# A conditional transformer block on one core: another order of VectorE's sums, and the first slot tile's rows computed apart

## The chip, the cores and the metric

The kernel runs on one core of a Trainium2 chip. The metric is the device time of one execution in microseconds (us), taken as the median over several runs. The profile is one more execution, traced instruction by instruction. Engines are named as in the profile: PE is TensorE (matmul, with its weight loads as PEld), DVE is VectorE, ACT is ScalarE, POOL is GpSimd, SP is SyncE, which here only issues DMAs.

## The reference

All data is float32: `x` is [32, 128, 512] (batch, token, feature), `cond` is [32, 512], the mask is [32, 128]. In short form:

```
shift, scale, gate = split(silu(t) @ ada_w + ada_b)          # per batch
norm = where(m, layernorm(x) * (1 + scale) + shift, 0)
ssm  = gelu(norm @ ssm_w1 + b1) @ ssm_w2 + b2  +  gelu(norm @ bwd_w1 + ..) @ bwd_w2 + ..   # exact gelu
x    = x + gate * where(m, ssm, 0)
shift, scale, gate = split(silu(t) @ ffada_w + ffada_b)
h    = gelu_tanh((layernorm(x) * (1 + scale) + shift) @ ff_w1 + ff_b1)     # 512 -> 1024
out  = x + gate * (h @ ff_w2 + ff_b2)                                      # 1024 -> 512
```

The flip of the sequence around the second network has no effect, since each token is treated alone. Only masked tokens go through the first half; in these inputs they are few.

## The kernel before, in words

**Order.** The whole body stands under a manual schedule: each engine runs its instructions in the order in which the code issues them. So where a line stands in the code, or under which key it is put in a table of fills, decides what it waits behind. Every wait is on a semaphore that the producing engine raises; an instruction that waits holds back all that follows on its engine.

**The head (up to about 84 us).** The masked tokens are counted on the chip and given 512 slots, four tiles of 128 (a loop at the end would take any further ones). The head computes the modulation rows `mod1` of all batches (PE, L309, copied out of PSUM by DVE in `modulation_rows`, L320), picks the rows of the first two slot tiles with matmuls (`of_slots`, L333: tile 0 and tile 1 in the same PSUM banks, one bank for each quarter of the features), and gathers the tokens of the slots. For each of the two tiles c = 0, 1 DVE then computes the mean and variance (L158, L159, L161), POOL the reciprocal root (L163), and DVE the modulated rows in two passes over four strips (`modulated_by_strips`, L347 and L351). Between the two tiles DVE also turns counts into the token numbers of the last two slot tiles (`counted`, L260 to L269), which read the result of two matmuls of `slots_to_count` (L254). PE transposes a tile in four steps (`transposed_slots`, L193) and ACT copies it to SBUF in two halves (L196). After a small transpose `ptr_b` (L684, L685), the first network's matmuls start (`ph_s`, L673). While PE has nothing to do in this stretch, it is given matmuls whose result nobody reads: `keep_clock(2, 0)` (L620, eight matmuls) and two with the identity (L647). SP issues the loads of the weights; `ssm_w1` is one load of 1 MB behind the first gather.

**The second half, four pairs.** The 32 batches are taken in NP = 4 pairs, each of two sides of G = 4 batches. Both matmul layers are done by a seven-product scheme of the Strassen kind, applied twice to the first layer. `FirstProduct` runs seven streams in the order 1, 2, 5, 6, 3, 7, 4, each with its products P5, P1, P3, P7, P2, P6, P4. A window (w = 1 to 6) interleaves the beginning of a new stream with the end of the old one. Each product is 4 passes of a 128x256 matmul in the trace (L1117). Each product goes into one of two accumulators, the banks `e` and `a`; DVE or ACT then reads the bank and forms the next partial sum. The DVE lines are:

- L1142, `seed`: e = a + an earlier result, at P1;
- L1147 (P7) and L1152 (P4): result = a + a stored part, into `hb`;
- L1161: e = a + p5 or a stored part, at P6.

PE can use the bank again only when that DVE line has read it. Line numbers as the profile has them: where a DVE line is the continuation of a statement, its number is that of the call.

**The token sums.** The streams 5, 6, 3, 7, 4 use sums and differences of blocks of the transposed input. `token_sums(j, n)`, j = 1 to 4, n = 0 to 3, forms them on DVE: j = 1 at L1046 (`sx`), j = 2 at L1050 (`xn_sy`), j = 3 at L1053 and j = 4 at L1056, both in place. In pair 0 all of j = 2 and (3, 0) stand ahead of the windows and the others at (2, 1) to (2, 6), that is, after the second to seventh product of window 2. In pairs 1 to 3 (2, 0) stands in the pair before, at the last step, and the others in windows 1 and 2.

**Beside them on DVE** stand the statistics of the next pair (`Statistics.one`, L917 and L918; `root`, L922, and on POOL L923), one small difference `fb2_step` (L1433), and after the windows `blocks(0, i)`: normalise a tile of the next pair (L929) and turn it in 32x32 blocks (L1479). POOL does the additions of the first layer (L1168, L1197, L1201) and issues the gathers of corrected tokens (`take_first_half`, L885). The second layer is `SecondProduct` (L1304) with steps in the order P1U, P5U, P1V, ... P4V; its `first_block` is DVE L1251.

The fills are put in by pairs of keys, window and product number:

```
for n, at in enumerate(((2, 1), (2, 3), (2, 3))):
    put(*at, now.token_sums, 3, 1 + n)
```

Of the kernel before, what the change touches and what calls it, by code (L numbers as in the profile page):

```python
# [9 lines left out]
F32 = mybir.dt.float32  # L10
# [12 lines left out]
def kernel(  # L23
# [111 lines left out]
    def load_behind_gathers(t, w):  # L135
        nc.gpsimd.memset(t[0:1, 0, 0:1], 0.0)
        load_blocks(t, w)
# [48 lines left out]
        nc.vector.scalar_tensor_tensor(t, t, stats[1], shift, ALU.mult, ALU.add)  # L186
        return t

    def transposed_slots(xn, dst, name):

        ptr = ps_t.tile([P, 512], F32, tag="tr", name=f"ptr_{name}")
        for k in range(KC):
            nc.tensor.transpose(ptr[:, ts(k, P)], xn[:, ts(k, P)], ident)  # L193
        for half_no in range(2):
            k = ts(half_no, KC // 2)
            nc.scalar.copy(dst[:, k], ptr.rearrange("p (k s) -> p k s", s=P)[:, k])  # L196

    def hidden(xT, n, w, bcol, func, name, pool, parts=range(HC), after=None):

# [47 lines left out]
            pick[:, part], slot_row[:, part], first, inside[:, part], ALU.is_ge, ALU.mult  # L247
        )

    def slots_to_count(picked, n, name, bank):  # L250

        pl = bank[0].tile([P, 512], F32, tag=bank[1], name=f"pl_{name}")
        for c in range(n):
            nc.tensor.matmul(pl[:, ts(c, S)], picked[:B, ts(c, P)], rank, start=True, stop=True)  # L254
        return pl[:, : n * S].rearrange("p (c s) -> p c s", s=S)

# [61 lines left out]
    def modulation_rows(pm, mod, lo, hi):  # L318
        view = pm[:, : (hi - lo) * P].rearrange("p (m c) -> p m c", c=P)
        nc.vector.tensor_copy(mod[:, lo:hi], view)  # L320

    def of_slots(picked, tiles, mod, kinds, banks, name):

        n = kinds.stop - kinds.start
        t = [
            pool.tile([P, 512], F32, tag=tag, name=f"{name}_{j}")[:, : len(tiles) * n * P].rearrange(
                "p (a m c) -> p a m c", m=n, c=P
            )
            for j, (pool, tag) in enumerate(banks)
        ]  # L330
        for at, c in enumerate(tiles):
            for j in range(KC):
                nc.tensor.matmul(  # L333
                    t[j][:, at],
                    picked[ts(j, B), ts(c, P)],
                    mod[ts(j, B), kinds],
                    start=(at == 0),
                    stop=True,
                    skip_group_check=True,
                )  # L340
        return t
# [243 lines left out]
    for c, bank in enumerate(((ps_o, "o"), (ps_t, "tr"))):  # L585
        if c:
            on_zeros(256)
        slot = slot_col[:, c : c + 1]
        token_c = tokens_of(pick[:, ts(c, P)], slot, 1, f"s0_{c}", ssm, bank)
        xc.append(both[:, c])  # L590
        gather(xc[c], token_c)
        if c == 0:
            load_behind_gathers(w1[:, :, :D], ssm_w1)
    load_behind_gathers(ada_a[:, :, 2 * D :], ada_w[:, 2 * D :])
    load_blocks(w1[:, :, D:], bwd_w1)
    raw = [x_tile(2 * n, 2) for n in range(2 * G // 2)]
# [31 lines left out]
    pm = ps_o.tile([P, 512], F32, tag="o", name="pm_ss")  # L628
    modulation_bias(pm, AT_A, 0, 2)
    modulation_matmuls(pm, ada_a, 0, 2, range(KC))  # L630
    slots_of_late = slots_to_count(pick[:, NH:], NC // 2, "s1", (ps_h, "h"))
    modulation_rows(pm, mod1, 0, 2)

    strips = of_slots(pick, (0, 1), mod1, slice(0, 2), 3 * [(ps_o, "o")] + [(ps_h, "h")], "part_s0")
    keep_clock(2, 0)
    xT_s = ssm.tile([P, KC, NH], F32, tag="xT", name="xT_s0", bufs=2)
    xT_t = ssm.tile([P, KC, NH], F32, tag="xT", name="xT_s1", bufs=2)
    xn = group_of_tiles("s")
    xn_s = []
    for c in range(2):  # L640
        mv, rstd = statistics(xc[c : c + 1], f"s{c}")
        xn_s.append(
            modulated_by_strips(xc[c], strips, c, xn[:, c], mv[:, 0, 0:1], rstd, xn[:, 2 + c])
        )
        if c == 0:
            for n in range(2):
                nc.tensor.matmul(  # L647
                    pm_keep_clock[:, ts(n, 2 * P)], ident, xn[:, 2, ts(n, 2 * P)], start=True, stop=True
                )
            token_i = counted(slots_of_late, slot_col[:, NC // 2 :], NC // 2, "s1", ssm)  # L650
    gather_slots(token_i)
    one_more_scale(AT_F)
    fw1 = fwp.tile([P, KC, FF], F32, name="fw1")
# [25 lines left out]
                skip_group_check=True,  # L679
            )  # L680

    transposed_slots(xn_s[0], xT_s[:, :, ts(0, P)], "s0")
# [737 lines left out]
    for n in range(2, 4):  # L1420
        now.token_sums(1, n)
    now.do(2, "P2", "P6")
    for n in range(4):
        now.token_sums(2, n)
    now.do(1, "P4")
    now.token_sums(3, 0)
    for p in range(NP):
        more_pairs = p + 1 < NP
        xs = x_of[p]
# [2 lines left out]
        def put(w, n, f, *args):  # L1432
            fills.setdefault(w, {}).setdefault(n, []).append(lambda: f(*args))  # L1433

        if p:
            for n, at in enumerate(((1, 3), (1, 4), (1, 6))):
                put(*at, now.token_sums, 2, 1 + n)
            put(1, 6, now.token_sums, 3, 0)
        for n, at in enumerate(((2, 1), (2, 3), (2, 3))):
            put(*at, now.token_sums, 3, 1 + n)  # L1440
        for n, at in enumerate(((2, 4), (2, 4), (2, 6), (2, 6) if more_pairs else (3, 1))):
            put(*at, now.token_sums, 4, n)
        put(3, 6, now.load_weights, 3)
        if p == 0:
            put(3, 6, load_rows_of_fw2, 0)
# [5 lines left out]
        second = SecondProduct(p, now.h, xs)  # L1451
        if p == 0:
            put(
                2, 0, nc.vector.tensor_tensor,
                fb2_step, fb2[:, D // 2 :], fb2[:, : D // 2], ALU.subtract,
            )
        put(6, 0, now.late_gelu, "11")
# [7 lines left out]
        if more_pairs:  # L1465
            x_next = x_of[p + 1]
            stats = [Statistics(x_next[side], f"{p + 1}_{side}") for side in range(2)]
            xn, xT = {}, {}

            def blocks(side, i):  # L1470

                if i == 0:
                    xn[side] = in_turned_blocks(
                        group_of_tiles(f"{p + 1}_0")
                        if side == 0
                        else sp.tile([P, G, D], F32, tag="s12", name=f"xn_{p + 1}_1")
                    )
# [48 lines left out]
        if more_pairs:  # L1526

            for i in range(G):
                put(2 + i // 2, blocks, 1, i)
            for k in range(KC):  # L1530
                put(4 + k // 2, lambda k: scaled(2 * (p + 1), xT[0], k), k)
                put(7 + k // 2, lambda k: scaled(2 * (p + 1) + 1, xT[1], k), k)
                if k == 1:
                    put(4, to_feature_rows, 1, nc.sync, nc.sync, nc.sync, nc.scalar)

            def begin(j):
                if j == 1:
# [12 lines left out]
            nxt = {}  # L1550
            put(10, next_product)
            put(11, lambda: nxt["p"].do(1, "P5", "P1"))
            for n in range(4):
                put(11 + n // 2, lambda n: nxt["p"].token_sums(1, n), n)
            put(13, lambda: nxt["p"].token_sums(2, 0))
            if p + 2 < NP:
                x_of[p + 2] = [[], []]
                put(11, lambda: x_of[p + 2][0].extend(load_side(p + 2, 0)))
            put(12, lambda: nxt["p"].do(1, "P2", "P6"))
            put(13, lambda: nxt["p"].load_weights(2))  # L1560
            if p + 2 < NP:
                put(13, lambda: x_of[p + 2][1].extend(load_side(p + 2, 1)))
# [128 lines left out]
```

## Time and profile before

| | us |
|---|---|
| median of 3 runs (456.37 to 456.99) | 456.78 |
| the profiled execution | 455.45 |
| its span, first to last instruction | 453.7 |
| PE busy, 2151 rows | 446.6 |
| DVE busy, 571 rows | 331.7 |
| ACT busy | 178.0 |
| POOL busy | 159.8 |

The profiled execution has 1.75 us around its span. The granted clock of TensorE has a mean of 0.999. In the timeline view each row gives the start, the duration, the engine, the line and operation, the operands and how many instructions were put together (x4); in brackets stands how long the engine had been idle before it and what ended that. The durations of matmul groups include their draining, so that the rate is read from start to start: a group of 4 passes that follows another without a pause starts 0.86 to 0.87 us after it.

### The profile page before, as it was taken

Reading aid. Unit: us, or ns where it says so; the run is one execution under the profiler, and the core shown is the slowest. Engines: PE = TensorE matmul, PEld = TensorE weight load, DVE = VectorE, ACT = ScalarE, POOL = GpSimd, SP = SyncE. Lnnn points to the kernel's source line nnn. Section 1 sums busy time; section 2 is a strip of 40 time slices with the busy share of each in tenths; the row PEclk is TensorE's granted clock in tenths of the full one; section 3 lists DMA queues with packets and bytes.
Section 4 is the critical chain, followed back from the end, with each engine's and each line's share of the span. In section 5 each row is a group of like instructions: output and inputs, shape, how many; then the busy total and the mean of one; then the engine's idle time right before and its main releaser. Section 6 shows DMA issues by size and latency. Waiting matters only on the chain.

```text
span 453.7 us, 6170 instructions
## 1 busy us (share of the span) xinstructions
PE 446.6 (98%) x2151; PEld 370.4 (82%) x2151; DVE 331.7 (73%) x571; ACT 178.0 (39%) x390; POOL 159.8 (35%) x154
## 2 busy tenths in 40 slices
PE   8999999999999999999999999999999999999996
PEld 3884585688888888888888888888888888888885
DVE  5798797697789759886796498867963995534645
ACT  3124127244642552446425514454355154552000
POOL 4220550089770000797700007977000027560000
PEclk9999999999999999999999999999999999999999
DMA  7999449745518817722187167221872442222023
GB/s 251 379 396 407 150 73 326 279 151 172 189 78 180 114 49 251 249 92 82 66 191 107 56 230 264 95 84 54 202 105 59 157 145 82 81 94 93 0 82 107
DMA packets 82611, 70.57 MB, mean 156 GB/s; under 512 B 63112, under 2 KB 63728, under 8 KB 81554
## 3 DMA queue, kind: packets, MB, share of 16 engines
q1 hardware_dynamic: 67762, 58.28, 40.9%
q0 software_dynamic: 4160, 10.54, 6.9%
q10 hardware_dynamic: 10656, 1.33, 2.1%
q8 instruction: 18, 0.29, 0.2%
q14 instruction: 15, 0.12, 0.1%
HBM read 56.46 MB, written 13.70 MB: 155 GB/s over the span
## 4 chain that ended last, share of the span: by engine, by line
PE 92%; DVE 5%; POOL 1%; issue 1%; ACT 1%; DVEq 0%
PE a_o L1304 23%; PE a_m L1117 18%; PE e_o L1304 18%; PE e_m L1117 14%; PE po_s L221 6%; PE ph_s L204 5%; PE ph_s L673 2%; PE pm_ss L309 1%; PE last L1304 1%; PE pm_f L309 1%; PE a_m_alone L1117 1%; PE pl_s L254 1%; DVE xn_sy L1050 0%; PE part_s L333 0%; DVE e_m L1142 0%
## 5 line engine op out<-in xcount | busy, mean ns | idle before, releaser
L1168 POOL TENSOR_TENSOR ha<-p_m,ha 128x512 f32<-128x512 f32 x20 | 25.8, 1289 | 178.8 <-ACT ha L1175 169.2
L1304 PE MATMUL e_o<-fw,ha 128*128 128x256 f32 x256 | 57.9, 379 | 0.0
L939 ACT ACTIVATE xT<-xT,modT 128x128 f32<-128x128 f32 x112 | 44.1, 480 | 31.6 <-DMA xT<-xn 31.4
L1304 PE MATMUL a_o<-t,hb 128*128 128x256 f32 x240 | 54.1, 379 | 0.0
L1304 PEld LDWEIGHTS e_o<-fw,ha 128*128 128x128 f32 x256 | 48.6, 190 | 6.6
L1304 PEld LDWEIGHTS a_o<-t,hb 128*128 128x128 f32 x240 | 45.6, 190 | 6.2
L1079 ACT ACTIVATE hb<-hb,biasT 128x256 f32<-128x256 f32 x64 | 29.0, 500 | 30.4 <-POOL hb L1201 19.8
L1131 ACT COPY p_m<-e_m 128x512 f32<-128x512 f32 x27 | 15.8, 586 | 47.8 <-PE e_m L1117 43.3
L885 POOL DMA_INDIRECT x<-x_rows,slot_i x24 | 29.2, 1218 | 6.0 <-issue 5.3
L1168 POOL TENSOR_TENSOR hb<-p_m,hb 128x512 f32<-128x512 f32 x20 | 29.6, 1481 | 0.3
L1304 PE MATMUL a_o<-fw,ha 128*128 128x256 f32 x128 | 28.9, 379 | 0.0
L1304 PE MATMUL a_o<-t,s 128*128 128x256 f32 x128 | 28.9, 379 | 0.0
L1304 PE MATMUL e_o<-fw,s 128*128 128x256 f32 x128 | 28.9, 379 | 0.0
L221 PE MATMUL po_s<-w,h_s 128*128 128x512 f32 x64 | 28.4, 594 | 0.0
L1175 ACT COPY ha<-e_m 128x512 f32<-128x512 f32 x32 | 18.5, 578 | 24.9 <-PE e_m L1117 24.6
L1304 PEld LDWEIGHTS a_o<-t,s 128*128 128x128 f32 x128 | 24.3, 190 | 3.3
L1304 PEld LDWEIGHTS a_o<-fw,ha 128*128 128x128 f32 x128 | 24.3, 190 | 3.3
L1304 PEld LDWEIGHTS e_o<-fw,s 128*128 128x128 f32 x128 | 24.3, 190 | 3.3
L1142 DVE TENSOR_TENSOR e_m<-a_m,ha 128x512 f32<-128x512 f32 x20 | 13.9, 696 | 17.0 <-POOL ha L1168 6.6
L1079 ACT ACTIVATE ha<-e_m,biasT 128x256 f32<-128x256 f32 x48 | 20.0, 468 | 14.8 <-PE e_m L1117 12.6
L1117 PE MATMUL a_m<-xT,tw 128*128 128x256 f32 x96 | 24.7, 380 | 0.4 <-DVE hb L1147 0.4
L1117 PE MATMUL e_m<-s,fw 128*128 128x256 f32 x92 | 23.8, 381 | 0.0
(237 smaller groups left out, 892.3 us busy)
## 6 DMA issues: line engine op xcount, KB each, us to landing
tw<-t_rows SPq DMA_DIRECT2D x16, 896.0 KB, 5.3
x<-in_x_dram SPq DMA_DIRECT2D x16, 512.0 KB, 8.8
gate<-gate_rows POOLq DMA_DIRECT2D x8, 1024.0 KB, 5.2
out_dram<-x SPq DMA_DIRECT2D x15, 512.0 KB, 4.9
xT<-xn SPq DMA_DIRECT2D x92, 64.0 KB, 2.4
ada_f<-in_L_cond_ffada_w_dram SPq DMA_DIRECT2D x4, 768.0 KB, 13.2
ada_a<-in_L_cond_ada_w_dram SPq DMA_DIRECT2D x4, 512.0 KB
w<-in_L_cond_ssm_w_dram SPq DMA_DIRECT2D x2, 1024.0 KB, 6.2
```

The costliest lines, as they stand in the source:

```text
L204: nc.tensor.matmul(ph[:, :n], w[:, k, ts(f, P)], xT[:, k, :], start=(k == 0), stop=(k == KC - 1))
L221: nc.tensor.matmul(po, h[f][:, ts(i, P)], w[:, f, :], start=(f == 0 and seeded is None), stop=(f == HC - 1), skip_group_check=seeded is no ...
L309: nc.tensor.matmul(pm[ts(j, B), : (hi - lo) * P], sT[:, k, :], kinds[:, k, lo:hi, ts(j, P)], start=False, stop=True, skip_group_check=True,)
L885: nc.gpsimd.indirect_dma_start(out=xs[i // G][i % G // 2][:, i % 2], out_offset=None, in_=x1_rows, in_offset=bass.IndirectOffsetOnAxis(ap= ...
L939: nc.scalar.activation(out, src, AF.Identity, bias=shift, scale=scale)
L1079: nc.scalar.activation(dst[:, n], src[:, n], AF.Gelu_apprx_tanh, bias=biasT[:, f : f + 1])
L1117: nc.tensor.matmul(bank[:, ts(n, QT)], self.w_block(j, product)[:, ts(n, P)], self.x_block(j, product), start=(product in ("P1", "P5") and ...
L1131: nc.scalar.copy(p5, e)
L1142: nc.vector.tensor_tensor(e, a, p5, add)
L1168: nc.gpsimd.tensor_tensor(self.place(RESULT[j], c), self.p5[j], other, ALU.add)
L1175: nc.scalar.copy(self.place(RESULT[j], c), src)
L1304: nc.tensor.matmul(part, src[:, k, ts(i, P)], w[product][:, k, :], start=(last and k == 0), stop=True, skip_group_check=True,)
```

## The change

In the head:

- The modulation rows are copied by ACT.
- The parts of slot tile 0 alone (`parts_of_tile(0)`, four matmuls) are issued between the two matmuls of `slots_to_count`, those of tile 1 after the transposes of tile 0.
- The transposes of tile 0 stand ahead of the work for tile 1, in two PSUM tiles of two transposes each, so that each of ACT's two copies has its own.
- `keep_clock` has four matmuls instead of eight, and the matmul with the identity stands once instead of twice.
- `ssm_w1` is loaded in two halves of 0.5 MB. SP so issues one DMA more.

In the pairs:

- The token sums of pair 0 are spread to later windows; in pairs 1 to 3 all of j = 2 stands in window 1, with nothing of it in the pair before.
- `fb2_step` moves from (2, 0) to (4, 1).
- The statistics of the next pair's side 0 move to later products, by one in pairs 1 and 2 and by three in pair 0; the root of side 0 moves from (3, 6) to (4, 1) in pairs 1 and 2, and one statistic of side 1 from (4, 6) to (5, 1).
- In pair 0, `blocks(0, 1)` moves behind the stream's P7.

On the engines this leaves DVE with one instruction fewer, ACT with one more, PE with five matmuls fewer (the keep-clock ones), and the number of POOL's unchanged.

```diff
-    def transposed_slots(xn, dst, name):
-        ptr = ps_t.tile([P, 512], F32, tag="tr", name=f"ptr_{name}")
+    def transposed_slots(xn, dst, name, apart=False):
+        ptr = [ps_t.tile([P, 512], F32, tag="tr", name=f"ptr_{name}")]
+        if apart:
+            ptr.append(ps_t.tile([P, 512], F32, tag="tr", name=f"ptr_{name}_1"))
         for k in range(KC):
-            nc.tensor.transpose(ptr[:, ts(k, P)], xn[:, ts(k, P)], ident)
+            nc.tensor.transpose(ptr[k // 2 % len(ptr)][:, ts(k, P)], xn[:, ts(k, P)], ident)
         for half_no in range(2):
             k = ts(half_no, KC // 2)
-            nc.scalar.copy(dst[:, k], ptr.rearrange("p (k s) -> p k s", s=P)[:, k])
+            t = ptr[half_no % len(ptr)]
+            nc.scalar.copy(dst[:, k], t.rearrange("p (k s) -> p k s", s=P)[:, k])
...
         for c in range(n):
+            if c and between:
+                between()
             nc.tensor.matmul(pl[:, ts(c, S)], picked[:B, ts(c, P)], rank, start=True, stop=True)
...
-            load_behind_gathers(w1[:, :, :D], ssm_w1)
+            load_behind_gathers(w1[:, :, : D // 2], ssm_w1[:, : D // 2])
+            load_blocks(w1[:, :, D // 2 : D], ssm_w1[:, D // 2 :])
...
-    slots_of_late = slots_to_count(pick[:, NH:], NC // 2, "s1", (ps_h, "h"))
-    modulation_rows(pm, mod1, 0, 2)
-    strips = of_slots(pick, (0, 1), mod1, slice(0, 2), 3 * [(ps_o, "o")] + [(ps_h, "h")], "part_s0")
-    keep_clock(2, 0)
+    def parts_of_tile(c):
+        strips_of[c] = of_slots(
+            pick, (c,), mod1, slice(0, 2), 3 * [(ps_o, "o")] + [(ps_h, "h")], f"part_s{c}"
+        )
+    nc.scalar.copy(mod1[:, 0:2], pm.rearrange("p (m c) -> p m c", c=P)[:, 0:2])
+    slots_of_late = slots_to_count(
+        pick[:, NH:], NC // 2, "s1", (ps_h, "h"), lambda: parts_of_tile(0)
+    )
+    keep_clock(1, 0)
...
+    modulated_slots(0)
+    nc.tensor.matmul(pm_keep_clock[:, : 2 * P], ident, xn[:, 2, : 2 * P], start=True, stop=True)
+    transposed_slots(xn_s[0], xT_s[:, :, ts(0, P)], "s0", True)
+    parts_of_tile(1)
+    token_i = counted(slots_of_late, slot_col[:, NC // 2 :], NC // 2, "s1", ssm)
+    modulated_slots(1)
...
-    for n in range(4):
+    for n in range(2):
         now.token_sums(2, n)
     now.do(1, "P4")
-    now.token_sums(3, 0)
...
+        sums = [(j, n) for j in (2, 3, 4) for n in range(4)]
         if p:
...
+            at_sums = (
+                (1, 1), (1, 3), (1, 4), (1, 6), (1, 6), (2, 1), (2, 3), (2, 3),
+                (2, 4), (2, 4), (2, 6), (2, 6) if more_pairs else (3, 1),
+            )
+        else:
+            sums = sums[2:]
+            at_sums = (
+                (2, 1), (2, 3), (2, 3), (2, 4), (2, 4), (2, 6), (3, 1), (3, 1), (3, 3), (3, 3),
+            )
...
-                2, 0, nc.vector.tensor_tensor,
+                4, 1, nc.vector.tensor_tensor,
                 fb2_step, fb2[:, D // 2 :], fb2[:, : D // 2], ALU.subtract,
...
-            for i, at in enumerate(((3, 1), (3, 3), (3, 4), (3, 6))):
+            for i, at in enumerate(((3, 1), (3, 3), (3, 4), (4, 1)) if p else ((3, 4), (3, 6), (4, 1), (4, 3))):
                 put(*at, stats[0].one, i)
-            put(*((3, 6) if p else (5, 4)), stats[0].root)
-            for i, at in enumerate(((4, 4), (4, 6), (5, 3), (6, 4))):
+            put(*((4, 1) if p else (5, 4)), stats[0].root)
+            for i, at in enumerate(((4, 4), (5, 1), (5, 3), (6, 4))):
...
-            for i in range(2):
+            for i in range(1 + (p > 0)):
                 blocks(0, i)
         now.do(4, "P3")
         second.seed(1)
         now.do(4, "P7")
+        if more_pairs and p == 0:
+            blocks(0, 1)
...
-            put(13, lambda: nxt["p"].token_sums(2, 0))
```

More of the change, by code (lines that the diff above doesn't have):

```diff
@@ L248, in pick_slots, with slots_to_count @@
         )
-    def slots_to_count(picked, n, name, bank):
+    def slots_to_count(picked, n, name, bank, between=None):
         pl = bank[0].tile([P, 512], F32, tag=bank[1], name=f"pl_{name}")
         for c in range(n):
+            if c and between:
+                between()
             nc.tensor.matmul(pl[:, ts(c, S)], picked[:B, ts(c, P)], rank, start=True, stop=True)
@@ L630 @@
     modulation_matmuls(pm, ada_a, 0, 2, range(KC))
-    slots_of_late = slots_to_count(pick[:, NH:], NC // 2, "s1", (ps_h, "h"))
-    modulation_rows(pm, mod1, 0, 2)
-    strips = of_slots(pick, (0, 1), mod1, slice(0, 2), 3 * [(ps_o, "o")] + [(ps_h, "h")], "part_s0")
-    keep_clock(2, 0)
+    strips_of = {}
+    def parts_of_tile(c):
[7 more added lines that the diff above has]
+    keep_clock(1, 0)
     xT_s = ssm.tile([P, KC, NH], F32, tag="xT", name="xT_s0", bufs=2)
@@ L639, with modulated_slots @@
     xn_s = []
-    for c in range(2):
+    def modulated_slots(c):
         mv, rstd = statistics(xc[c : c + 1], f"s{c}")
         xn_s.append(
-            modulated_by_strips(xc[c], strips, c, xn[:, c], mv[:, 0, 0:1], rstd, xn[:, 2 + c])
+            modulated_by_strips(xc[c], strips_of[c], 0, xn[:, c], mv[:, 0, 0:1], rstd, xn[:, 2 + c])
         )
[L645 to L650, printed above, removed]
+    modulated_slots(0)
[4 more added lines that the diff above has]
+    modulated_slots(1)
     gather_slots(token_i)
@@ L680, in hidden_of_tile @@
             )
-    transposed_slots(xn_s[0], xT_s[:, :, ts(0, P)], "s0")
     ptr = ps_t.tile([P, 512], F32, tag="tr", name="ptr_b")
@@ L1433, in put @@
             fills.setdefault(w, {}).setdefault(n, []).append(lambda: f(*args))
+        sums = [(j, n) for j in (2, 3, 4) for n in range(4)]
         if p:
[L1436 to L1442, printed above, removed]
+            at_sums = (
[7 more added lines that the diff above has]
+            )
+        for at, of in zip(at_sums, sums):
+            put(*at, now.token_sums, *of)
         put(3, 6, now.load_weights, 3)
```

## The prediction

> **What bounds the kernel now.** The page's first part and its chain that ended last are read first.
>
> ```profile
> PE 446.6 (98%) x2151; PEld 370.4 (82%) x2151; DVE 331.7 (73%) x571; ACT 178.0 (39%) x390; POOL 159.8 (35%) x154
> ...
> PE 92%; DVE 5%; POOL 1%; issue 1%; ACT 1%; DVEq 0%
> ```
>
> TensorE is busy 98% of the span and makes 92% of the chain. So only its remaining pauses, or matmuls taken from its queue while nothing else holds it, can give time. Such a pause is short, so the second view is the waits of PE: it names `a_m L1117 <- DVE hb L1147` with 0.7 us in two waits. Busy time hides more than this, so the third view is PE's timeline, read from start to start: a group of 4 passes should start 0.865 us after the one before.
>
> ```profile
> 97.75 1.03 PE L1117 MATMUL a_m<-sx,tw 128*128 128x256 f32 x4
> 99.00 1.13 PE L1117 MATMUL a_m<-xT,t 128*128 128x256 f32 x4 [0.23 <-DVE hb L1147]
> 99.97 1.03 PE L1117 MATMUL e_m<-xn_sy,tw 128*128 128x256 f32 x4
> 100.83 1.03 PE L1117 MATMUL a_m<-xn_sy,tw 128*128 128x256 f32 x4
> 101.75 1.13 PE L1117 MATMUL e_m<-sx,tw 128*128 128x256 f32 x4
> 102.72 1.03 PE L1117 MATMUL a_m<-sx,tw 128*128 128x256 f32 x4
> 103.88 1.13 PE L1117 MATMUL e_m<-xn_sy,tw 128*128 128x256 f32 x4
> ```
>
> Three groups come late: 99.00 by 1.25 - 0.865 = 0.39, 101.75 by 0.06, 103.88 by 0.30. The group after each pause also takes 0.97 instead of 0.865 to its successor, 0.10 more each time. Together: 0.39 + 0.06 + 0.30 + 3 x 0.10 = **1.05**. What came late is on DVE's timeline:
>
> ```profile
> 96.73 0.68 DVE L1053 TENSOR_TENSOR s<-s 128x512 f32<-128x512 f32 x1
> 97.33 0.41 DVE L1433 TENSOR_TENSOR fb_step<-fb 128x256 f32<-128x256 f32 x1
> 97.67 0.67 DVE L1053 TENSOR_TENSOR xT<-xT 128x512 f32<-128x512 f32 x1
> 98.27 0.67 DVE L1147 TENSOR_TENSOR hb<-a_m,hb 128x512 f32<-128x512 f32 x1
> ...
> 102.81 0.41 DVE L1056 TENSOR_TENSOR s<-s,xn_sy 128x256 f32<-128x256 f32 x1
> 103.14 0.68 DVE L1161 TENSOR_TENSOR e_m<-a_m,ha 128x512 f32<-128x512 f32 x1
> ```
>
> DVE has no pause from 91.65 to 108.3. The read of PE's bank (L1147, L1161) stands behind token sums and `fb2_step`, and PE starts 0.06 us after that read ends (98.94 to 99.00, 103.82 to 103.88).
>
> **The change part by part.**
>
> *Pair 0, token sums.* Eight sums (7 of them 0.67 or 0.41 long) leave the stretch from 95 to 103, `fb2_step` (0.41) too. Up to the L1147 of 98.27 DVE had four sums of j = 2 (0.68, 1.28 for two, 0.41), three of j = 3 and `fb2_step` since 94.59, 3.7 us of work behind each other. In the new order only (2,0) and (2,1) (about 1.3) and two or three more stand before it, and PE's product for it ends at about 97.0: the read goes then, 1.2 us earlier. The L1161 of 103.14 likewise stands behind at most two sums per product, about 1.2 us against the 0.865 to 1.73 us that PE gives between two reads. So all three pauses go: **-1.05**. The sums are wanted later than they come: the latest, (4,3) at (3,3), is read by a stream that starts a window (7 x 0.865 = 6 us) later. The statistics of side 0 (four of 0.68 + 0.18) that move back fall where DVE waits 0.6 to 1.05 us for others at a time (rows at 110.23, 112.79, 116.34). The same holds for `fb2_step`, which is first read by the `seed` of the second layer more than 15 us later.
>
> *Pair 0, `blocks(0, 1)`.* A second place of the same kind:
>
> ```profile
> 129.89 3.62 PE L1304 MATMUL e_o<-fw,s 128*128 128x256 f32 x16
> 133.93 1.13 PE L1117 MATMUL a_m<-xT,tw 128*128 128x256 f32 x4 [0.42 <-DVE hb L1147]
> ```
>
> 16 passes are 4 x 0.865 = 3.46, so 133.35 was due and 133.93 came: 0.58, and 0.10 behind it. DVE's L1147 (133.22, 0.65 long) stands behind two normalisations and two turns (130.07 to 133.2). With only one pair ahead of it it starts at about 131.3 and ends at 132, before PE asks: **-0.68**. The moved pair (1.27 + 0.64) then runs from 132 to 134, and the L1152 of 135.59 is behind it as before. The chain for the next pair (DVE's turned rows, SP's DMAs, ACT, DVE's L986) ends at 166.83 and PE takes it at 169.59, 2.8 us of slack, of which PE's own gain takes little, since DVE's last turned row moves with PE.
>
> *Pairs 1 to 3.* At 206.59 to 207.63, 297.55 to 298.58 and 364.30 to 365.35 PE waits for the L1161 of 206.89, 297.85 and 364.61; each interval is 1.04, 1.03 and 1.05, so 0.17 + 0.17 + 0.18 late and 0.10 behind each. In pairs 1 and 2 a statistic (206.07 and 297.03, 0.68 + 0.18) stands ahead of it, in pair 3 (2,0) at 364.00 (0.68). All three are moved behind: **-0.82**. The root of the next pair's side 0 moves on POOL behind two L1168 (1.26 each); the sum that follows (L1197, 203.58) comes at the same time, as the three only change places. The whole of j = 2 in window 1 is done there between reads, where in pairs 1 and 2 DVE waits 0.9 to 1.8 us (rows at 201.58 and 204.87).
>
> *The head.*
>
> ```profile
> 12.35 1.02 PE L333 MATMUL part_s<-mod,pick 32*128 32x256 f32 x13
> 13.41 1.12 DVE L347 SCALAR_TENSOR_TENSOR xn_s<-xc,mv_s,part_s 128x128 f32<-128x128 f32 x4 [0.38 <-PE part_s L333]
> ...
> 16.46 3.81 PE L673 MATMUL ph_s<-xT_s,w 128*128 128x128 f32 x32 [0.27 <-issue]
> ```
>
> DVE waits for the last of eight matmuls (13.37). ACT's copy of the rows costs 0.37 (its rows at 20.75) where DVE's took 0.42, so the parts may start at 12.0; four of the eight end 0.6 earlier, at 12.8. L347 then starts 0.58 earlier, and so the transposes. From there PE has the parts of tile 1 (4 matmuls; eight take 1.07 at 25.99, so 0.54 to 0.64) and `ptr_b` between the transposes and L673, where it had only `ptr_b`. With the transposes' end at about 15.3 these end at 15.9 and `ptr_b` at 16.15. The matmul chain wants the first of ACT's two copies only, and this waits for two transposes instead of four (15.3 instead of 15.99). So L673 starts at 16.15: **-0.31**; bounds are -0.58 (nothing added on PE's path) and +0.1 (parts of tile 1 wait for the strips of tile 0). The five keep-clock matmuls taken away (0.13 to 0.28 each) fell into waiting time and give nothing. The DMA more costs SP 0.43 to 0.68 of issue (rows at 15.96 and 10.00); `ssm_w1`'s bytes are the same, and the second half is wanted 1.8 us after the first, so nothing. `counted` moves from before L158 of tile 1 to the same place after tile 0: nothing; tile 1's rows are ready at 19.0 and wanted at 19.8.
>
> Sum: -1.05 - 0.68 - 0.82 - 0.31 = **-2.86**. Not every wait can go entirely, as POOL's case below says; I take -2.8. The profiled execution's 455.45 becomes 452.65. It lies 1.33 below the median of the runs, 456.78, which so becomes **454.0**. About 0.2% (0.91 us) is what a measurement of this kernel can tell from no change: below 455.87 counts as faster.
>
> **A rule against it.** In pair 0 the gathers of POOL at 99.89 and 102.26 take 2.07 and 1.83 against 1.00 for others, and L1168 1.71 (92.08) against 1.27, each while DVE adds two SBUF tensors; DVE's own sum at 92.58 takes 1.48 against 0.42. [...]
>
> **Rivals.**
>
> *A: POOL takes DVE's place in pair 0.* POOL works without a pause from 93.94 to 114. L1142 at 112.79 follows POOL's L1197 (111.48 + 1.27 = 112.75), and PE takes its bank at 114.35 with 0.8 us to spare. If PE comes 1.05 earlier and POOL doesn't, PE waits 0.27 there, and 0.10 behind it: -2.49, 454.3. If moved sums also slow POOL's additions (0.44 each, as at 92.08, in three of them), all of pair 0's 1.05 is handed back: -1.81, 455.0. For it: the unbroken row. Against it: the gathers get shorter when DVE's sums leave them (2 x 0.9).
>
> *B: the wait goes to the next in line.* DVE's work is the same in sum; what is moved delays another bank read as much. Then pairs 0 to 3 give nothing and blocks(0, 1) its 0.68: 456.1, no change. Against it: DVE waits at most of the places to which work moves.
>
> *C, slower: TensorE's clock.* Less filler in the head: PE has pauses of about 0.3 each near 13.5 and 14. If the granted clock fell to half there, all of PE's work from 14.3 to 20.1 (0.93 + 1.00 by the windows to 16.5, 3.60 to 20.1) would take twice as long: +5.5 - 2.86 = +2.7, 459.4. It decides from 2.9 us of matmuls at half the clock. Against it: PE's weight loads show 0.90 without work at 10.45, and the windows from 11.3 to 16.5 and to 20.1 have 1.00. [...]
>
> **How the numbers follow.** Forecast (453.2 to 454.3): 0.55. A (454.3 to 455.2): 0.23. B (455.9 to 456.5): 0.11. C: 0.06. The other 0.05: half of it gains above 3.5 (the -0.58 of the head's bound, waits that I count at nothing), half a loss of unknown place. The range 453.0 to 455.6 holds forecast and A with their bounds. Faster: 0.55 + 0.23 + 0.025 = 0.81; same 0.11; slower 0.08.
>
> **What would show it.** In the changed kernel: no gap over 0.9 between groups of 4 passes near 98 to 104 and 133, the L1161 of pairs 1 to 3 directly behind L1152, L673 at about 16.15, clock 1.00 from 11 to 20. A shows as a new wait of PE near 113 for L1142 with POOL's L1197 before it. Wrong would be: the same intervals of 1.05 to 1.25 at other places, or a later L673.

## The result, and the profile after

The changed kernel takes 460.72 us (median of 6 runs, 458.79 to 461.95), the kernel before in the same comparison 456.31 (6 runs, 455.51 to 456.99): ratio **1.009**, 95% interval 1.0072 to 1.0108. By this ratio it is slower by about 4.1 us (the medians lie 4.4 apart); forecast were 454.0 and a range of 453.0 to 455.6. The profiled execution took 460.46, its span is 458.7 beside 453.7 of before, 5.0 more.

One correction to the text on record: in the description of the kernel before, L1142 and L1161 are exchanged (L1161 is `seed` at P1, L1142 the sum at P6); no number depends on it.

In the changed kernel these lines stand 14 further down: the read at P7 is L1161 (L1147 before), `seed` L1175, the sum at P6 L1156, the sums of j = 4 L1070; POOL's additions are L1182 and L1211, its gathers L899. In experiments with two lines added, L1211 is L1213 and `fb2_step` (L1446) is L1448. The views leave out numbers in tile names, so `fb2_step` reads `fb_step`.

The page, its first part and the chain that ended last:

```profile
PE 448.9 (98%) x2141; PEld 371.3 (81%) x2141; DVE 337.2 (74%) x570; ACT 178.9 (39%) x391; POOL 160.1 (35%) x154
...
PE 72%; DMA 8%; DVE 5%; SPq 4%; ACT 4%; POOL 4%; issue 3%; ACTq 0%; POOLq 0%; DVEq 0%
```

DVE has one instruction fewer than before and is busy 5.5 us longer (331.7 before): something made single instructions longer. PE has lost 20 points of the chain. PE's waits name the place:

```profile
PE a_m L1131 <- DVE hb L1161: 3.1, 1, 3.1
```

PE's timeline there (start, duration, operation, in brackets the idle time before it):

```profile
97.96 1.03 PE L1131 MATMUL a_m<-sx,tw 128*128 128x256 f32 x4
98.82 1.03 PE L1131 MATMUL a_m<-xT,t 128*128 128x256 f32 x4
99.68 1.03 PE L1131 MATMUL e_m<-xn_sy,tw 128*128 128x256 f32 x4
...
103.14 1.03 PE L1131 MATMUL e_m<-xn_sy,tw 128*128 128x256 f32 x4
104.00 1.03 PE L1131 MATMUL a_m<-xn_sy,tw 128*128 128x256 f32 x4
108.15 2.08 PE L1131 MATMUL a_m<-sx,tw 128*128 128x256 f32 x4 [3.12 <-DVE hb L1161]
110.02 1.53 PE L1131 MATMUL e_m<-s,fw 128*128 128x256 f32 x4
111.39 1.03 PE L1131 MATMUL a_m<-xT,fw 128*128 128x256 f32 x4
```

The three pauses between 98 and 104 are gone, as forecast. Then 4.15 us lie between two starts where 0.865 were due, and the two groups behind take 1.87 and 1.37 each. DVE and POOL in the same stretch:

```profile
101.68 0.70 DVE L1175 TENSOR_TENSOR e_m<-a_m,ha 128x512 f32<-128x512 f32 x1
102.29 4.61 DVE L1070 TENSOR_TENSOR s<-s,xn_sy 128x512 f32<-128x512 f32 x1
106.82 0.68 DVE L1070 TENSOR_TENSOR xT<-xT,xn_sy 128x512 f32<-128x512 f32 x1
107.42 0.68 DVE L1161 TENSOR_TENSOR hb<-a_m,p_m 128x512 f32<-128x512 f32 x1
```

```profile
101.47 1.12 POOL L899 DMA_INDIRECT x<-x_rows,slot_i  x1 [0.30 <-issue]
102.62 1.28 POOL L1182 TENSOR_TENSOR ha<-p_m,ha 128x512 f32<-128x512 f32 x1
103.84 1.28 POOL L1182 TENSOR_TENSOR hb<-p_m,hb 128x512 f32<-128x512 f32 x1
105.07 1.26 POOL L1211 TENSOR_TENSOR ha<-ha 128x512 f32<-128x512 f32 x1
106.49 1.30 POOL L899 DMA_INDIRECT x<-x_rows,slot_i  x1 [0.16 <-issue]
```

The sum (4,0) takes 4.61 us where its like takes 0.68. It begins under a gather, and ends 0.57 us (106.90) after the last of three POOL additions (106.33), which themselves take 1.26 to 1.28 each, as three in a row did in the kernel before (104.11 to 107.83). The windows view (stretch, length, busy time with count for PE, PEld, DVE, ACT, POOL, granted clock, DMA share, GB/s) shows the second part of the price, a granted clock of 0.50 behind the pause:

```profile
105.00:108.00 3.00, 0.03 (x1) 0.00 (x0) 3.00 (x3) 0.00 (x0) 2.63 (x3) 0.94 0.00 0
108.00:109.00 1.00, 0.85 (x2) 0.76 (x3) 1.00 (x4) 0.00 (x0) 0.00 (x0) 0.50 0.12 33
109.00:110.00 1.00, 1.00 (x3) 0.75 (x3) 0.97 (x4) 0.00 (x0) 0.00 (x0) 0.50 0.00 0
110.00:111.00 1.00, 1.00 (x4) 0.80 (x3) 1.00 (x2) 0.59 (x1) 0.00 (x0) 0.50 0.00 0
111.00:112.00 1.00, 1.00 (x6) 0.90 (x5) 0.25 (x2) 0.36 (x1) 0.00 (x0) 0.99 0.80 151
```

**Where the 5.0 us come from**, by the start of the same matmul in both traces (minus is earlier than before). The table compares one execution of each kernel:

| place (time before) | step, us | stands at |
|---|---|---|
| head, L673 at 16.46 | -0.66 | -0.66 |
| 34 to 39.4: gates, second matmuls of the first half | +0.87 | +0.21 |
| pair 0 to 104.2: the three pauses | -1.06 | -0.85 |
| 105.7: wait for the held sum | +3.29 | +2.44 |
| 105.7 to 107.4: half clock | +1.51 | +3.95 |
| up to 118.7 | +0.32 | +4.27 |
| 133.9: `blocks(0, 1)` | -0.69 | +3.58 |
| 134.9: seed of the second layer | +0.49 | +4.07 |
| pair 1: 203.1 and 207.6 | +0.25, -0.31 | +4.01 |
| pair 2: 294.1 and 298.6 | +0.24, -0.30 | +3.95 |
| pair 3: 351 to 370 | +1.03 | +4.98 |

### The profile page after: what moved, and what is told of

Read it like the earlier page. It is cut to its first block, busy times and chain, and to the rows that moved or that the text cites. A ratio compares the mean times of both kernels' runs of the same rounds, so it can differ in the third digit from the quotient of the medians.

```text
span 458.7 us, 6152 instructions
## 1 busy us (share of the span) xinstructions
PE 448.9 (98%) x2141; PEld 371.3 (81%) x2141; DVE 337.2 (74%) x570; ACT 178.9 (39%) x391; POOL 160.1 (35%) x154
## 3 DMA queue, kind: packets, MB, share of 16 engines
q10 hardware_dynamic: 10656, 1.33, 2.1%
## 4 chain that ended last, share of the span: by engine, by line
PE 72%; DMA 8%; DVE 5%; SPq 4%; ACT 4%; POOL 4%; issue 3%; ACTq 0%; POOLq 0%; DVEq 0%
PE a_m L1131 17%; PE a_o L1318 17%; PE e_m L1131 14%; PE e_o L1318 13%; PE po_s L224 5%; DMA w<-in_L_cond_bwd_w_dram 4%; SPq L970 3%; PE ph_s L207 3%; DMA ada_a<-in_L_cond_ada_w_dram 2%; DMA xT<-xn 1%; ACT xT L953 1%; POOL hb L1215 1%; PE last L1318 1%; PE a_m_alone L1131 1%; POOL ha L1215 1%
## 5 line engine op out<-in xcount | busy, mean ns | idle before, releaser
L1182 POOL TENSOR_TENSOR ha<-p_m,ha 128x512 f32<-128x512 f32 x20 | 26.3, 1317 | 182.8 <-ACT ha L1189 169.1
L953 ACT ACTIVATE xT<-xT,modT 128x128 f32<-128x128 f32 x112 | 44.2, 480 | 34.6 <-DMA xT<-xn 34.0
L1182 POOL TENSOR_TENSOR hb<-p_m,hb 128x512 f32<-128x512 f32 x20 | 29.8, 1492 | 0.3
L899 POOL DMA_INDIRECT x<-x_rows,slot_i x24 | 27.8, 1159 | 6.0 <-issue 5.3
L1093 ACT ACTIVATE ha<-e_m,biasT 128x256 f32<-128x256 f32 x48 | 20.1, 469 | 14.9 <-PE e_m L1131 13.5
L1156 DVE TENSOR_TENSOR e_m<-a_m,ha 128x512 f32<-128x512 f32 x20 | 13.9, 697 | 14.3 <-POOL ha L1182 6.6
```

The costliest lines, as they stand in the source:

```text
L899: nc.gpsimd.indirect_dma_start(out=xs[i // G][i % G // 2][:, i % 2], out_offset=None, in_=x1_rows, in_offset=bass.IndirectOffsetOnAxis(ap= ...
L953: nc.scalar.activation(out, src, AF.Identity, bias=shift, scale=scale)
L1093: nc.scalar.activation(dst[:, n], src[:, n], AF.Gelu_apprx_tanh, bias=biasT[:, f : f + 1])
L1156: nc.vector.tensor_tensor(e, a, p5, add)
L1182: nc.gpsimd.tensor_tensor(self.place(RESULT[j], c), self.p5[j], other, ALU.add)
```

## The experiments

**Theory 1:** POOL's additions hold a VectorE sum that reads two SBUF tensors, and the new order in pair 0 brings such a sum to them. **Theory 2:** the time is lost in the head or the later pairs, or the sum waits for something of its own. Ratios are against the kernel before, run beside each.

**Pair 0 as before, all else changed.** The sums, `fb2_step` and side 0's statistics of pair 0 get their old places; the first five of these sums (`sums[:5]`) stand ahead of the windows again:

```diff
...
-            sums = sums[2:]
-            at_sums = (
-                (2, 1), (2, 3), (2, 3), (2, 4), (2, 4), (2, 6), (3, 1), (3, 1), (3, 3), (3, 3),
-            )
+            sums = sums[5:]
+            at_sums = ((2, 1), (2, 3), (2, 3), (2, 4), (2, 4), (2, 6), (2, 6))
...
```

> The changed kernel, with the order of pair 0's token sums, of fb2_step and of its side-0 statistics as before; all else as changed. Theory 1 (POOL's additions hold a VectorE sum that reads two SBUF tensors): the sum (4,0) no longer meets three additions in a row, so the 4.61 us row at 102.29 is gone, and with it 3.29 us of PE pause and 1.5 us at half the clock; the 1.05 us that the order had gained before that place are lost. 460.7 - 4.8 + 1.05 = 457.0, with no L1070 row over 1 us and a granted clock of 1.00 from 84 to 160. Theory 2 (the head or the later pairs cost the time): stays near 460.

Measured: 455.97 beside 455.96, ratio 0.9993 (0.9979 to 1.0008), clock 1.00, no L1070 row above 1 us in pair 0. The whole loss is in pair 0's order. All other parts of the change together are worth nothing that can be measured. I had expected 457.0, which is 0.7 above the 456.31 of the kernel before; no such difference was measured.

**Pair 0's order alone, on the kernel before** (the same edit the other way round; the sums of j = 4 are L1056 here).

> The kernel before with only pair 0's order of token sums, fb2_step and side-0 statistics as in the change. Theory 1: the same meeting of (4,0) with three additions: -1.05 + 3.3 + 1.5 = +3.7 on 456.3, so 460.0, with one L1056 row of 3 to 5 us and a stretch of half clock behind it. Theory 2 (head or later pairs): about 455.3 with no such row.

Measured: 460.83 beside 455.96, ratio 1.0121 (1.0085 to 1.0156). Its L1056 at 102.20 takes 4.59 us, PE's wait is 3.1 and the clock 0.50 from 109 to 111. Both directions agree.

**Gathers between the additions.** DVE's order is that of the change; one gather moves between the two L1182 of stream 6, one ahead of L1211:

```diff
             nc.gpsimd.tensor_tensor(self.place(RESULT[j], c), self.p5[j], other, ALU.add)
+            if self.p == 0 and j == 6 and c == "12":
+                take_first_half(1, x_of[1], range(G + 1, G + 2))
...
-            put(2, 6, take_first_half, p + 1, x_next, range(G, G + 2))
-            put(3, 4, take_first_half, p + 1, x_next, range(G + 2, G + 3))
+            put(2, 6, take_first_half, p + 1, x_next, range(G, G + 2 if p else G + 1))
+            put(3, 4 if p else 2, take_first_half, p + 1, x_next, range(G + 2, G + 3))
```

> The changed kernel with VectorE's order untouched; of POOL's gathers in pair 0 one is put between its two L1182 additions of stream 6, and one before its L1211, so that no two additions stand next to each other there. Theory 1: the sum (4,0) gets through in the first gap, after one addition at most: its row takes 0.7 to 1.9 us instead of 4.61, PE's pause is under 0.4, the clock stays at 1.00: 460.7 - 4.5 = 456.2 (455.8 to 457.0). Theory 2 (the sum is held by something that it alone waits for, such as its operands or a load into SBUF in that stretch): the row stays at 4.6 and the time at 460.7.

Measured: 459.14, ratio 1.0061 (1.0040 to 1.0083): half right. DVE's timeline, and POOL's behind it:

```profile
101.38 1.12 DVE L1070 TENSOR_TENSOR s<-s,xn_sy 128x512 f32<-128x512 f32 x1
...
108.39 3.02 DVE L1448 TENSOR_TENSOR fb_step<-fb 128x256 f32<-128x256 f32 x1
```

```profile
104.86 1.29 POOL L899 DMA_INDIRECT x<-x_rows,slot_i  x1 [0.16 <-issue]
106.17 1.29 POOL L1213 TENSOR_TENSOR ha<-ha 128x512 f32<-128x512 f32 x1
107.40 1.28 POOL L1182 TENSOR_TENSOR ha<-p_m,ha 128x512 f32<-128x512 f32 x1
108.62 1.27 POOL L1182 TENSOR_TENSOR hb<-p_m,hb 128x512 f32<-128x512 f32 x1
109.85 1.26 POOL L1213 TENSOR_TENSOR ha<-ha 128x512 f32<-128x512 f32 x1
```

The sum (4,0), the first row, gets through in 1.12 instead of 4.61, as theory 1 says and theory 2 denies. But now another sum with two SBUF inputs, the moved `fb2_step`, meets the next run of additions, and is held until they end (111.11): 3.02 instead of 0.41. PE waits 2.0 us for the read behind it, and the clock is 0.50 from 113 to 116.

**Both holds taken away:** the edit above, and `fb2_step` early, where POOL is idle:

```diff
     for n in range(2):
         now.token_sums(1, n)
+    nc.vector.tensor_tensor(fb2_step, fb2[:, D // 2 :], fb2[:, : D // 2], ALU.subtract)
     now.apart(1)
...
-        if p == 0:
-            put(
-                4, 1, nc.vector.tensor_tensor,
-                fb2_step, fb2[:, D // 2 :], fb2[:, : D // 2], ALU.subtract,
-            )
```

> The changed kernel with POOL's gathers between its additions as above, and fb2_step early (behind the first two token sums), so that neither (4,0) nor fb2_step meets a run of additions. Theory 1: the pause of 2.0 us at 112.86, the slow clock behind it and the 0.4 us at 107.10 go too, and the whole loss of the change with them: 455.2, between 454.5 and 456.0, granted clock 1.00 from 84 to 160, no two-input sum over 1.8 us. Rival (pair 0's new order costs something else besides): above 456.5.

Measured: 455.35 beside 455.86, ratio 0.9984 (0.9957 to 1.0011). The loss of the change is gone with the two holds; what is left of its gain is within the noise.

**The sums of j = 4 later.** The four go from (3,1) and (3,3) to (3,3) and (3,4), behind the bank read.

> The changed kernel with the four sums of j = 4 of pair 0 put one or two products later: (4,0) and (4,1) behind the bank read at (3,3), (4,2) and (4,3) at (3,4). Theory 1: the sums start while POOL's additions run already (102.6 to 106.3). If additions in a row hold any sum until the last of them is done, (4,0) still ends at about 106.9, but the bank read is ahead of it, so PE loses only what stands behind: the next read of a bank or the sum itself, wanted at about 105.7; 458 to 459.5. If a sum takes turns with the additions, as at 92.29 to 94.3, each of the four takes 1.0 to 1.8 us, the last ends near 107.5: 456.5 to 457.5. Theory 2 (held by its operands): a row near 4.6 or none, at no fixed place against POOL.

Measured: 457.46, ratio 1.0035 (1.0017 to 1.0054). The sum (4,0) starts at 104.62, 0.10 us into the second of three additions, and is held 2.95 us, to 0.57 after the third:

```profile
104.62 2.95 DVE L1070 TENSOR_TENSOR s<-s,xn_sy 128x512 f32<-128x512 f32 x1
```

So in both traces the hold ended with the run of additions (0.57 us behind its end), whether the sum began 0.33 us ahead of the first of them or 0.10 into the second. The bank read is ahead of it, PE waits 0.9 and 1.1 us in two pieces, and the clock stays at 1.00. The time lies in the range that I had given for sums that take turns (456.5 to 457.5) and below the one for the hold (458 to 459.5); the row of 2.95 us decides for the hold.

**Do sums and additions take turns or not?** Elsewhere in the same traces they do (in the kernel before `sx` at 92.58 takes 1.48 us instead of 0.42, and the L1168 beside it 1.71 instead of 1.27). Three kernels measure it: behind step 3 of the second layer POOL gets a run of additions, released by one DVE instruction, and DVE four instructions beside it (all in addition to the kernel before). They ran once each, and only their rows are read. The first:

```diff
...
+                nc.vector.tensor_tensor(met, fb2, fb2, ALU.add)
+                for _ in range(6):
+                    nc.gpsimd.tensor_tensor(met, met, fb2, ALU.add)
+                for n in range(4):
+                    if p == 0:
+                        nc.vector.tensor_tensor(by[:, :256], fb2[:, 256:], fb2[:, :256], ALU.subtract)
+                    elif p == 1:
+                        nc.vector.tensor_scalar(by[:, :256], fb2[:, :256], 1.0, None, ALU.add)
+                    else:
+                        nc.vector.bn_stats(st, fb2)
...
```

> The kernel before with added work that leaves the output as it is: behind step 3 of the second layer in pairs 0, 1 and 2 POOL does six additions in a row (128x512, two SBUF inputs, released by one VectorE instruction), and VectorE four instructions beside them: in pair 0 sums with two SBUF inputs (128x256, 0.41 us alone), in pair 1 one-input tensor_scalars of that size, in pair 2 one-input statistics (0.68 alone). Theory 1 (POOL's additions in a row hold a sum with two SBUF inputs): in pair 0 the first sum lasts until the sixth addition ends, about 7.6 us, and the additions take 1.26 each; if instead they take turns, each of the four sums takes 1.0 to 1.7 and the additions about 1.7. In pair 2 neither engine is slowed. For pair 1 I have no firm expectation: 0.3 us each if one input never meets, or held as in pair 0 if it does.

```profile
143.74 4.64 DVE L1574 TENSOR_TENSOR by<-fb 128x256 f32<-128x256 f32 x4
...
238.08 4.28 DVE L1576 TENSOR_SCALAR by<-fb 128x256 f32<-128x256 f32 x4
...
331.91 2.88 DVE L1578 BATCH_NORM_STATS2 st_met<-fb 128x6 f32<-128x512 f32 x4
```

Theory 1 in my form is wrong here: they take turns. Three of the four sums took 1.37 instead of 0.42, each let in when an addition ended. The one-input `tensor_scalar` meets the additions in the same way (1.27 to 1.32 instead of 0.29), the statistics don't (0.69, as long as elsewhere). Each of these additions waited for the one before.

> As the measurement of the meeting above (which left the output as it is, and showed gaps of 0.08 us between POOL's additions, each of which waited for the one before, and a sum let in at each gap), but with additions that don't wait for each other: six in pair 0, two in pair 1, three in pair 2, each with four sums of two SBUF inputs (128x256) beside them. If the gap decides, the first sum lasts until the last addition ends: about 7.6 us with six, 2.5 with two, 3.8 with three. If it doesn't, the sums take 1.3 to 1.7 each as before, and what held (4,0) is something of its own place.

Additions alternating between two targets (`(to_a, to_b)[n % 2]`) gave the same: 4.69, 3.74 and 4.64 us for the four sums beside six, two and three additions. The gap doesn't decide.

The third puts a gather directly ahead of the additions in pairs 0 and 1, as there was one ahead of every run that had held a sum:

> As the two measurements of the meeting before (the output is as before), with one thing more that the held sums of pair 0 had: POOL's run of additions stands directly behind a gather, which in pairs 0 and 1 goes into a scratch tile, so that its first addition waits for nothing; six additions in pair 0, three in pair 1. In pair 2 a very small POOL instruction stands there instead. VectorE has one statistic of 0.68 and then four sums (128x256). If the gather ahead decides, the first sum in pairs 0 and 1 is held until the last addition ends (up to 7.6 and 3.8 us), and in pair 2 sums and additions take turns at 1.3 to 1.5. If they take turns everywhere, what lets a sum in between two additions stays open.

DVE's and POOL's timelines, pair 0, and DVE's in pair 1 (three additions) and pair 2 (no gather):

```profile
145.70 9.50 DVE L1587 TENSOR_TENSOR fb_step<-fb 128x256 f32<-128x256 f32 x4
...
244.90 5.81 DVE L1587 TENSOR_TENSOR fb_step<-fb 128x256 f32<-128x256 f32 x4
...
341.19 5.49 DVE L1587 TENSOR_TENSOR fb_step<-fb 128x256 f32<-128x256 f32 x4
```

```profile
145.47 1.10 POOL L1573 DMA_INDIRECT by<-x_rows,slot_i  x1 [9.35 <-DVE by L1571]
146.60 1.28 POOL L1584 TENSOR_TENSOR to_a<-met,fb 128x512 f32<-128x512 f32 x1
...
152.72 1.27 POOL L1584 TENSOR_TENSOR to_b<-met,fb 128x512 f32<-128x512 f32 x1
```

```profile
340.92 1.25 POOL L1584 TENSOR_TENSOR to_a<-met,fb 128x512 f32<-128x512 f32 x1
342.14 1.44 POOL L1584 TENSOR_TENSOR to_b<-met,fb 128x512 f32<-128x512 f32 x1
```

Behind a gather the additions run at 1.26 to 1.28 and one sum is held to the end of the run: 8.14 us with six additions (from 146.14 to 0.29 behind the last), 4.46 with three. Without the gather, in pair 2 of the same kernel, each sum takes 1.27 to 1.37, and the additions behind the first (1.25) take 1.44 to 1.46: they take turns. A gather that lay further back did not make the additions hold a sum: in the changed kernel `fb2_step` (113.16) began in the first of POOL's next additions (112.31, after an idle time of 4.53 us on POOL) and took 0.71, let in when that addition ended. One exception stands against a strict rule: in the first of the three kernels a sum at 196.61 began just after an addition that followed a gather, and was let in after 1.1 us. What makes the difference inside the chip stays open.

**The head alone**, on the kernel before.

> The kernel before with only the head of the change. Theory 1 (the head's gain of 0.67 us at the first network's matmuls is handed back where PE next waits for a load, near 34 to 39 us, since the DMA queues run without a pause there): 456.0, between -0.3 and +0.4 of the kernel before. Theory 2 (the gain is kept to the end): 455.3.

Measured: 456.99 beside 456.44, ratio 1.0011 (0.9993 to 1.0029). A gain of 1 us that is kept to the end (theory 2) is ruled out; the end that theory 1 has (-0.3 to +0.4) lies within the interval. The place at which I had it lost doesn't: in this trace L673 comes 0.67 earlier, 0.28 of it goes at the gates' matmuls, 0.39 is still there at 84 us and 0.08 at 385, and PE doesn't wait for the load near 39 us.

**`fb2_step` early, alone** (the one-line edit above, and its old place empty).

> The kernel before with one VectorE instruction moved: fb2_step goes from (2,0) of pair 0 to behind the first two token sums, where VectorE waits 2 us for PE and POOL is idle. It removes 0.41 us from VectorE's queue ahead of the bank reads, so PE's pauses of 0.39 + 0.06 + 0.30 and the slow group behind each should go, without any token sum meeting POOL's additions: -0.8 to -1.05, 455.0, no L1056 row over 1 us. Rival: the reads were late for another reason than this 0.41, or POOL's additions come late instead: less than 0.3 gained.

Measured: 456.05 beside 456.44, ratio 0.9994 (0.9980 to 1.0009): by this ratio 0.27 us are gained, and the interval reaches from 0.9 gained to 0.4 lost. The rival had said less than 0.3. In the trace the first pause shrinks from 0.39 to 0.06, but the third stays 0.30. DVE has no pause in that stretch, so 0.41 taken from its queue helps once, not at each read. And a new pause stands ahead of it, which takes back what the first one gave; it is also in the traces of the two better versions below, and not in that of the kernel before:

```profile
89.55 1.13 PE L1117 MATMUL e_m<-s,fw 128*128 128x256 f32 x4 [0.36 <-DVE e_m L1142]
```

What makes this read of the bank late was not tried.

**A better version:** that, and of the change only the sums of pairs 1 to 3, the statistic of side 1 at (5,1) and `blocks(0, 1)` behind P7; then also the sums (4,2) and (4,3) of pair 0 from (2,6) to (3,6).

> The kernel before with fb2_step early as in the run above, and of the change only what I count as harmless: in pairs 1 to 3 all of j = 2 in window 1, one statistic of side 1 from (4,6) to (5,1), and in pair 0 blocks(0,1) behind P7. The root stays where it was. -1.0 for pair 0, -0.28 twice and -0.29 for the pairs, -0.3 to -0.4 for the blocks (the seed of the second layer is late next): -1.9 to -2.2, 454.0. Rival: the pairs' waits only move on, -1.0 to -1.3, 454.8.

> The best kernel so far (455.05 beside 456.44) with the sums (4,2) and (4,3) of pair 0 at (3,6) instead of (2,6), where POOL's three additions should be over or nearly so. It takes 1.08 us of sums out of the stretch in which VectorE sets PE's pace, so PE's pauses near 101.5 and 103.6 (0.06 + 0.30, and 0.10 behind each) go: -0.5, 454.5. If the additions aren't over when (4,2) starts, it is held until they are, at most 1.26 us, and PE waits about 0.5 us instead: 455.3.

Measured: 455.05 beside 456.44, ratio 0.9964 (0.9947 to 0.9982), and with the two sums later **454.34 beside 455.86, ratio 0.9952** (0.9926 to 0.9979). DVE's timeline of the second:

```profile
106.14 0.70 DVE L1142 TENSOR_TENSOR e_m<-a_m,ha 128x512 f32<-128x512 f32 x1
106.74 0.94 DVE L1056 TENSOR_TENSOR xT<-xT,xn_sy 128x512 f32<-128x512 f32 x1
107.61 0.41 DVE L1056 TENSOR_TENSOR s<-s,xn_sy 128x256 f32<-128x256 f32 x1
```

The moved sum meets only the end of the last addition (107.13) and costs 0.94 instead of 0.68; PE's group at 103.69 comes 0.86 after the one before, so the third pause is gone. Both beat the kernel before and the change. The two intervals overlap, so the times don't tell what the two later sums add. In its traced execution the first version lost 1.06 us at 385.96, where PE waited for the weights `tw` (a DMA). That is most of what this execution had gained by then. The same wait stands in the traces of `fb2_step` early (0.82) and of pair 0's order alone (0.52), and not in those of the kernel before, the change or the second version; what decides it was not tried.

## Why the prediction was wrong

- **Pair 0, the pauses: right.** Forecast -1.05, measured -1.06. The way in which DVE's queue was read held.
- **Pair 0, where the sums go: the step that failed.** I wrote that the sums "are wanted later than they come" and so costed their new places at nothing in the sum. Rival A did name POOL's additions there, but let the meeting cost at most the 1.05 that the order had gained. I had not asked whether one sum can wait for several additions. The kernel before had its sums beside gathers, two of which took 2.07 and 1.83 there against 1.00 to 1.42 for the others; the change put (4,0) at 102.29, ahead of three additions behind a gather, and it was held 4.61 us. The wait for it cost PE 3.29, and the half clock behind it cost 1.51: +4.80, where the sum had 0. Undoing this part brings the ratio from 1.009 to 0.9993, doing it alone gives 1.0121.
- **A smaller misreading in the same paragraph:** eight sums were to leave the stretch from 95 to 103. Eleven sums began there before, and eight still do. The three pauses went even so, since the sums now stand behind the bank reads.
- **Rival A: the right neighbour, the wrong mechanism and size.** It had POOL in pair 0 as the bound and additions slowed by 0.44 each, giving back 1.05 at most. It was the sum that paid (4.61 us instead of 0.68), not the additions (1.26 to 1.28), and for all three at once; behind a gather and six additions one sum paid 8.14 us. I used the addition of 1.71 at 92.08 to bound a loss of gain and no loss beyond it, though the row at 92.58 (1.48 instead of 0.42) already showed a sum that waits until an addition ends.
- **Rival C: the right effect in the wrong place.** The head kept its clock (1.00 from 11.3 to 20.1 in the changed kernel too). The half clock (0.50 from 107.6 to 111.0) came in pair 0, behind a pause of 3.12 us that the prediction didn't have.
- **The head: not kept, and not measured well by one trace.** In this execution L673 came 0.66 earlier instead of 0.31 (0.27 of it because the last wait for the conditioning weights, 10.45, was shorter), and by 39.6 PE stood 0.21 later than before. Of the 0.87 between, 0.50 came at the gates' matmuls (34.2 to 34.6), whose cause was not followed, and 0.38 at a load:

```profile
18.91 20.12 DMA w<-in_L_cond_bwd_w_dram
39.03 0.04 issue
39.07 3.27 PE po_s L224 x7
```

  PE waits for the second matmuls' weights, which land 20.12 us after their issue. The sum had no term for a later load; it only priced the second half of `ssm_w1` at nothing. No other kernel's trace has this wait. The start of L673 (L688 with the new head) lies at 15.39 to 17.31 in the traces that have the new head and at 15.71 to 16.76 in those that have the old, so a step of 0.3 can't be read from one execution of each; the times of the head alone (1.0011, 0.9993 to 1.0029) show no gain.
- **`blocks(0, 1)`: -0.69 against -0.68, then +0.49.** ACT's seed of the next accumulator was late next (a wait of 0.23 behind `a_o` L1257), which I had not named.
- **Pairs 1 and 2: -0.31 and -0.30 against -0.28, then +0.25 and +0.24.** The root moved into POOL's additions, and its little DVE instruction, 0.15 to 0.34 in the kernel before, takes 1.10 and 1.09 there and ends 0.04 behind an L1182 in both (206.64, 297.53). Pair 1:

```profile
205.58 1.10 DVE L936 TENSOR_SCALAR ve<-mv 128x4 f32<-128x4 f32 x1
206.59 0.68 DVE L1161 TENSOR_TENSOR hb<-a_m,hb 128x512 f32<-128x512 f32 x1
```

  The better versions, with the root in its old place, keep the gain there. I had counted the root on POOL and not on DVE.
- **Pair 3: +1.03 against -0.29 in this execution.** The pause shrank by 0.09 instead of going, and 1.12 came in new ones from 351 on. DVE's block sums for that pair (L1000, at 353.97) wait 7.42 us for ACT's rows, where they waited 6.03 before. In the kernel with the gathers between the additions, whose later pairs are the same, this wait is 6.31, the pause shrinks by 0.30, and pair 3 stands at -0.08 in all. There the forecast step held, and what it gave was mostly lost at other places of the pair. What made ACT's rows late in the changed kernel stays open.

## What to carry to other kernels

Before a VectorE sum with two SBUF inputs is moved, lay POOL's timeline beside its new place. In the kernel before two gathers beside such sums took 2.07 and 1.83 us against 1.00 to 1.42 for the others of pair 0; in the changed kernel one sum waited for a whole run of three POOL additions (4.61 us against 0.68), and so did the bank read behind it on VectorE, for which PE waited 3.12. A place where VectorE had waited was not free while POOL was adding there (`fb2_step` in the kernel with the gathers between the additions, 3.02 us against 0.41). Time that is won on the bounding engine may count only up to the next load or copy that was just in time (of the head's 0.66 us, 0.38 went at the load at 39.07), so follow each gain to the next wait before it enters the sum.

## What the hardware showed that I had not expected

- A two-input sum of 0.40 us took 8.14 us behind a gather and six POOL additions, 4.46 behind three; without the gather, 1.27 to 1.41 and the additions 1.33 to 1.48 instead of 1.26.
- A `tensor_scalar` with one SBUF input met POOL's additions too (1.27 to 1.32 instead of 0.29); statistics with one input didn't (0.69).
- Behind one pause of PE of 2.03 us (the kernel with gathers between the additions) the granted clock stood at 0.50 for about 3.4 us (113.0 to 116.4). With one of 3.12 us in the changed kernel it did the same from 107.6 to 111.0, which began 2.6 us into the pause. Two of 0.9 and 1.1 with work between them left it at 1.00. What sets off the slow stretch was not followed further.
